# Attention on one Trainium2 core: a finished chunk's projection matmul issued right behind the matmuls of the denominators, ahead of the two copies out of PSUM

## The chip, the cores and the metric

The kernel runs on one core of a Trainium2 chip. The five engines of the core are named as in the profile: PE is the matrix engine (TensorE), with its weight loads shown apart as PEld; DVE is VectorE; ACT is ScalarE; POOL is GpSimd; SP is the queue that issues most transfers. The metric is device time in microseconds of one execution of the whole program; the time of a kernel is the median of its runs.

## The reference, cut to what matters

The program is a two-layer network on an image batch of 4 x 64 x 64 positions with 128 channels. Layer 0 is attention followed by a recurrent network over the tokens; layer 1 is a convolution with a selective scan followed by a mixture of experts. Only the attention is touched by the change. It computes, for each image `b` with its 4096 positions as a sequence, four heads of 32 channels:

```
q, k, v = split(einsum('bxyc,cf->bxyf', layernorm(x), w_qkv))
q, k    = l2norm_axis1(q), l2norm_axis1(k)
sim     = einsum('bihd,bjhd->bhij', q, k) * 10.0
attn    = softmax(sim, axis=-1)
out     = einsum('bhij,bjhd->bhid', attn, v)
out     = einsum('bxyd,dc->bxyc', out, w_out) + b_out
x       = x + out
```

So for every query position the exponentials of 4096 scores are needed for each head, their sum (the denominator), their weighted sum of `v` (the numerator), the quotient, and then a projection by `w_out`, a bias and the residual.

## The kernel before

Everything is in float32. Channels lie on the 128 partitions, so a head is a strip of 32 partitions. The kernel first normalizes and prepares `q`, `k` and `v` of the four images, stores them, and then runs the attention stage proper, `attend` (its stage of the profile lies between about 225 and 2726 us). A chunk is 512 query positions of one image; there are 8 chunks in each of 4 images, 32 in all. For each chunk the keys are walked in 32 tiles of 128 keys (`t`, up to `NJ` = 32), each with four heads (`i`). One unit is the score matmul of one tile and one head: 128 keys by 512 queries, one PSUM bank.

The stage is written under a manual schedule: each engine executes its instructions in the order in which the Python loop emits them. The loop works in turns. One turn does the following.

- `scores("sa", 4)` (L286, L301): four score matmuls into the PSUM tile `sa` (four banks, one buffer), then one exponential on ACT of all four banks (128 x 2048) into a ring in SBUF. The ring holds eight tiles of four heads.
- Either a second `scores("sb", 3)` into the PSUM tile `sb` (three banks, one buffer), with an exponential of 128 x 1536; or, in a counting turn, other use of the same `sb` tile, called `slot`.
- `weighted` (L310): for up to two finished tiles, four matmuls each that multiply the exponentials by `v` and accumulate in the PSUM bank `av`. After the last tile of a chunk ACT copies `av` to `o` (L319).
- `added` (L329, L333): DVE adds each finished tile of exponentials, 128 x 2048, to a running `total`; after eight tiles the `total` is complete and is put on the list `to_count`, due three turns later (`LATER`).
- The list `later` of the previous turn: small DVE operations whose inputs came from ACT in that turn.
- `divided` (L352, L353): when a chunk's denominators are complete, DVE takes the reciprocal and multiplies `o` by it; the chunk then goes on the list `to_project`.

A counting turn is what the change touches. `counted` (L338 to L348) issues four matmuls by a matrix of ones, one for each head, which sum `total` over the 128 keys of the partition dimension into bank 0 of `slot`; ACT then copies this bank to `den` (L345 for the first count of a chunk, L347 for the three others, whose DVE addition goes on `later`). If a chunk waits on `to_project`, the same turn calls `projected` (L355 to L366): it issues the load of the chunk's piece of `x` on the SP queue (L358), the projection matmul by `wo` of the finished `o` into bank 1 of the same `slot` (L359), and ACT's copy of that bank with the bias added (L360); the addition of the residual (L363) and the store (L364) go on `later`. The turn in which a chunk is projected is the first counting turn of the next chunk, so that its copy is the one of L345. The last chunk has no such turn: it is projected alone at the end. There are therefore 31 turns with both, and one with a projection only.

Waits between engines are put in by the framework. It follows dependencies by whole tiles: `slot` is one tile, so two accesses of it by different engines, of which one is a write, are put in the order in which they were emitted, even where they lie in different banks. In the program before, the projection matmul waits for ACT's copy of `slot`, and the biased copy waits for the projection matmul.

## Time and profile before

The kernel before takes 10372.5 us, the median of 3 runs (10369.3 to 10379.58). The profiled execution took 10381.96 us, with a span of 10379.9 us from the first instruction to the last.

| what | value |
|---|---|
| profiled execution, its span | 10381.96 us, 10379.9 us |
| median of 3 runs, lowest, highest | 10372.5 us, 10369.3 us, 10379.58 us |
| mean granted PE clock over the span | 0.966 |
| attention stage, window 240 to 2740 us: PE, DVE, ACT busy | 2340.03, 2246.10, 1970.55 us of 2500 |
| its granted PE clock | 0.99 |
| projection matmuls L359 | 64 instructions (two for each of 32 projections), 346.2 to 2722.7 us |
| copies L345 of the first count of a chunk | 32, median 578 ns |
| biased copies L360 | 32, median 689 ns |

In the lines of the profile, `L359` is a line of the kernel, the engine's name stands before it, and `out<-in` names the tiles. In the timeline a line gives the start in us, the duration in us, the instruction with the number merged into it, and in brackets the idle time of its engine before it with what ended it. `32*128` or `128*32` beside a matmul is the part of the PE array, rows by columns, that one instruction uses. A matmul in float32 appears as two PE instructions. The list of waits gives total us, times, and the longest wait.

### The profile page before, as it was taken

How to read it: one execution, taken by the hardware profiler on the slowest of the kernel's cores; microseconds unless marked ns; L12 is line 12 of the kernel's file. 1: busy time of each engine (PE TensorE's matmuls, PEld its weight loads, DVE VectorE, ACT ScalarE, POOL GpSimd, SP SyncE). 2: the span in 40 equal slices, each digit the busy share in tenths (PEclk: the TensorE clock that was granted, in tenths of full speed). 3: DMA queues.
4: the chain of work that ended last, by engine and by line, in shares of the span. 5: the costliest groups of instructions: out<-in, count | busy, mean ns of one | idle time of the engine just before them, and what ended most of it. 6: DMA issues, size and time to landing. Idle time of an engine off the chain costs nothing.

```text
span 10379.9 us, 244130 instructions
## 1 busy us (share of the span) xinstructions
PE 9318.5 (90%) x103920; PEld 4400.3 (42%) x103920; DVE 8856.0 (85%) x8023; ACT 6815.2 (66%) x9682; POOL 5616.8 (54%) x3513
## 2 busy tenths in 40 slices
PE   7999999999888869999999999999999999999766
PEld 3222222222233335555555555555555555555323
DVE  7999999999685159999999999999999999999864
ACT  3778777777564557777776776776777766767311
POOL 0000000000011159999999999999999999999300
PEclk8999999999999979999999999999999999999877
DMA  4000000000212335555655565655565555566634
GB/s 181 7 7 31 9 31 7 9 7 8 86 61 93 125 118 139 144 153 149 154 146 139 143 158 148 151 146 136 144 158 153 144 141 144 146 149 157 203 131 167
DMA packets 529249, 1173.61 MB, mean 113 GB/s; under 512 B 47954, under 2 KB 436634, under 8 KB 498330
## 3 DMA queue, kind: packets, MB, share of 16 engines
q1 hardware_dynamic: 528154, 1157.87, 40.1%
q8 instruction: 827, 13.55, 0.5%
q14 instruction: 268, 2.20, 0.1%
HBM read 816.74 MB, written 190.00 MB: 97 GB/s over the span
## 4 chain that ended last, share of the span: by engine, by line
DVE 49%; issue 8%; PE 4%; DMA 2%; DVEq 1%; POOL 0%; ACT 0%; SPq 0%; POOLq 0%; ACTq 0%
DVE states L1255 41%; DVE db L1248 3%; DVE b_diag L1139 1%; DVE log L1111 1%; PE db L1217 1%; DMA weights<-in_w 1%; PE y L1308 1%; DVEq L1255 0%; DVE y L1446 0%; PE norm_mean_ps L115 0%; PE x_ps L1065 0%; DVEq L1248 0%; PE gate_ps L1536 0%; PE pool_ps L1566 0%; PE norm_var L121 0%
## 5 line engine op out<-in xcount | busy, mean ns | idle before, releaser
L1255 DVE TENSOR_TENSOR_SCAN states<-decays,db 128x920 f32<-128x920 f32 x2304 | 4761.9, 2067 | 175.9 <-DVE db L1248 4.6
L1279 POOL TENSOR_TENSOR products<-states,c_ring 128x912 f32<-128x912 f32 x2304 | 4513.7, 1976 | 437.7 <-DVE db L1248 167.8
L1193 ACT ACTIVATE decays<-dt,a_logs 128x456 f32<-128x456 f32 x4608 | 3100.2, 676 | 97.6
L1217 PEld LDWEIGHTS db<-b_diag,dtu_t 32*128 32x128 f32 x18432 | 2233.7, 187 | 1790.5 <-issue 1332.6
L1217 PE MATMUL db<-b_diag,dtu_t 32*128 32x128 f32 x18432 | 2636.8, 282 | 374.4 <-DVE states L1255 308.7
L1217 PE MATMUL db<-b_other,dtu_t 32*128 32x128 f32 x18432 | 2674.5, 284 | 5.6 <-DMA b_other<-b_diag 3.1
L1226 PE MATMUL y<-zeros 32*128 32x128 f32 x17224 | 2496.4, 283 | 5.4 <-issue 5.3
L1308 PE MATMUL y<-products,ident 64*64 64x456 f32 x18432 | 2314.2, 570 | 9.4 <-issue 7.0
L1217 PEld LDWEIGHTS db<-b_other,dtu_t 32*128 32x128 f32 x18432 | 2236.3, 187 | 8.6 <-issue 4.7
L1226 PEld LDWEIGHTS y<-zeros 32*128 32x128 f32 x17224 | 2085.4, 187 | 7.4 <-issue 7.3
L333 DVE TENSOR_TENSOR total<-total,ring 128x2048 f32<-128x2048 f32 x768 | 1759.3, 2291 | 76.0 <-ACT ring L301 10.4
masks.py:197 POOL MEMSET ident<- 128x128 f32 x6 | 1.2, 205 | 3154.3 <-SPq L177 2840.7
L301 ACT ACTIVATE ring<-sa 128x2048 f32<-128x2048 f32 x640 | 1203.7, 1881 | 467.3 <-PE sa L286 467.3
L1266 ACT COPY carry<-states 128x8 f32<-128x8 f32 x576 | 117.7, 204 | 1677.6 <-DVE states L1255 1627.0
L310 PE MATMUL av<-ring,v_at 128*32 128x512 f32 x8192 | 1010.0, 599 | 0.1
L286 PE MATMUL sa<-q_at,k_at 32*128 32x512 f32 x5120 | 731.8, 641 | 61.2 <-ACT ring L301 36.1
L301 ACT ACTIVATE ring<-sb 128x1536 f32<-128x1536 f32 x512 | 741.4, 1448 | 0.0
L1308 PEld LDWEIGHTS y<-products,ident 64*64 64x64 f32 x18432 | 493.3, 131 | 334.5 <-issue 54.9
L286 PE MATMUL sb<-q_at,k_at 32*128 32x512 f32 x3072 | 555.3, 615 | 50.7 <-ACT ring L301 50.7
L310 PEld LDWEIGHTS av<-ring,v_at 128*32 128x32 f32 x8192 | 210.4, 109 | 700.9 <-issue 676.3
L1248 DVE COPY db<-states 128x8 f32<-128x8 f32 x1728 | 302.9, 175 | 205.8 <-PE db L1217 25.2
L286 PEld LDWEIGHTS sa<-q_at,k_at 32*128 32x128 f32 x5120 | 200.3, 183 | 616.7 <-ACT ring L301 310.0
(208 smaller groups left out, 9178.6 us busy)
## 6 DMA issues: line engine op xcount, KB each, us to landing
c_ring<-c_rows SPq DMA_DIRECT2D x576, 912.0 KB, 7.5
b_other<-b_diag SPq DMA_DIRECT2D x288, 512.0 KB, 9.6
u<-u_r SPq DMA_DIRECT2D x72, 456.0 KB, 10.4
y_r<-sum SPq DMA_DIRECT2D x72, 456.0 KB, 4.3
u<-u_c SPq DMA_DIRECT2D x72, 456.0 KB, 10.4
y_c<-sum SPq DMA_DIRECT2D x72, 456.0 KB, 4.7
weights<-in_w SPq DMA_DIRECT2D x32, 1024.0 KB, 12.9
x<-x SPq DMA_DIRECT2D x96, 256.0 KB, 2.7
```

The source lines that it names most:

```text
L286: nc.tensor.matmul(s[:, m, :], k[rows, tokens(t)], q[rows, chunk(chunk_state["c"])], start=True, stop=True,)
L301: nc.scalar.activation(ring[:, lo : lo + n, :], s[:, at : at + n, :], AF.Exp)
L310: nc.tensor.matmul(chunk_state["av"][rows, :], chunk_state["v"][:, t, rows], ring[:, at + i, :], start=t == 0, stop=t == NJ - 1,)
L333: nc.vector.tensor_add(total, total, w)
L1193: nc.scalar.activation(to, dt, AF.Exp, scale=scale)
L1217: nc.tensor.matmul(bank.rearrange("p (n t) -> p n t", n=4)[:, :, at : at + 32], v.dtu[rows, h, s, :], b[rows, s, 4 * self.q : 4 * self.q + ...
L1226: nc.tensor.matmul(y[:, idle // 2, :P], zeros[rows], zeros[rows], start=False, stop=False)
L1248: nc.vector.tensor_copy(self.edge(self.db[:, SKIP:], v.into), self.edge(before.slot(states), v.outof) if self.nth else self.carry(),)
L1255: nc.vector.tensor_tensor_scan(order(self.slot(states)), order(self.slot(decays, 1 if self.v.back else 0)), order(self.db[:, SKIP:][:, : 2 ...
L1266: nc.scalar.copy(self.carry(), self.edge(self.slot(states), self.v.outof))
L1279: nc.gpsimd.tensor_mul(to, h, c)
L1308: nc.tensor.matmul(to, ident[rows, rows], of, start=begins, stop=ends)
```

## The change

In the kernel before, one counting turn with a projection emits: four count matmuls, ACT's copy to `den`, the load of `x`, the projection matmul, ACT's biased copy. In the changed kernel it emits: four count matmuls, the load of `x`, the projection matmul, ACT's copy to `den`, ACT's biased copy. `counted` now ends after its matmuls and returns its copy as a function, `taken`; `projected` ends after its matmul and returns its biased copy as `biased`; the loop calls both after both matmuls have been emitted. A turn that only counts, and the last projection, emit the same instructions in the same order as before.

```
                 nc.tensor.matmul(
                     slot[DH * i : DH * i + DH, 0, :], ones, total[:, i, :], start=True, stop=True
                 )
+            return lambda: taken(slot, chunk_state, t)
+
+        def taken(slot, chunk_state, t):
             if t < SUMMED:
                 chunk_state["den"] = work.tile([P, 2, CH], F32, tag="den", name="den")
             den = chunk_state["den"]
...
             nc.tensor.matmul(slot[:, 1, :], wo, chunk_state["o"], start=True, stop=True)
-            nc.scalar.activation(x[:, 1, :], slot[:, 1, :], AF.Identity, bias=bo)
+
+            def biased():
+                nc.scalar.activation(x[:, 1, :], slot[:, 1, :], AF.Identity, bias=bo)
+                later.append(kept)
...
-            later.append(kept)
+            return biased
...
                 slot = ps.tile([P, 3, CH], F32, tag="sb", name="sb")
+                after = []
                 if counting:
                     _, chunk_state, t, total = to_count.pop(0)
-                    counted(slot, chunk_state, t, total)
+                    after = [counted(slot, chunk_state, t, total)]
                     if t == NJ - 1:
                         to_divide.append(chunk_state)
                 if to_project:
-                    projected(slot, to_project.pop(0))
+                    after.append(projected(slot, to_project.pop(0)))
+                for step in after:
+                    step()
```

In the built programs the order of the instructions on each single engine is the same in both kernels. What differs is the waits of 31 turns. The projection matmul no longer waits for ACT. ACT's copy to `den` now waits for the projection matmul (one more PE completion than before), and the biased copy behind it no longer waits for PE. Two waits of the following score matmuls, which the projection's old wait had covered, are now written out: `sa` on the exponential before the copy, `sb` on PE.

## The prediction

> **What bounds the kernel now.** The printed chain of work that ended last is no help for this change: it names no line of the attention stage, and its shares by engine add up to about 64% of the span. I therefore read the stage itself. The table of windows comes first: the attention stage, without its ends, in stretches of 500 us.

> ```profile
> core 0: us, PE busy (x) PEld busy (x) DVE busy (x) ACT busy (x) POOL busy (x), PEclk, DMA share, GB/s
> ...
> 500.00:1000.00 500.00, 470.60 (x3530) 125.45 (x3534) 452.21 (x220) 396.80 (x273) 0.00 (x0) 1.00 0.06 21
> ```

> PE is busy 94% of the time at full clock, DVE 90%, ACT 79%. PE leads, but DVE is close behind, so the question is whether time that PE gets back is also time that DVE has. The list of waits of the stage (240 to 2730 us) says where PE stands still for the edited lines:

> ```profile
> DVE total L329 <- ACT ring L301: 175.6, 97, 22.6
> ...
> PE sb L359 <- ACT den L345: 45.8, 31, 1.5
> ACT x_at L360 <- PE sb L359: 44.8, 32, 7.1
> ```

> PE waits 31 times for the copy to `den` before the projection, 45.8 / 31 = 1.48 us each. ACT then waits for the projection. DVE waits for exponentials about once per chunk-quarter of eight tiles, so it doesn't set the pace. Then the timeline of one engine at a time. PE in a counting turn without a projection, and in one with it:

> ```profile
> 614.44 1.14 PE L286 MATMUL sa<-q_at,k_at 32*128 32x512 f32 x8
> 615.51 1.07 PE L338 MATMUL sb<-total,ones 128*32 128x512 f32 x8
> 616.39 1.90 PE L310 MATMUL av<-ring,v_at 128*32 128x512 f32 x16
> 618.22 1.14 PE L286 MATMUL sa<-q_at,k_at 32*128 32x512 f32 x8
> ...
> 651.71 1.14 PE L286 MATMUL sa<-q_at,k_at 32*128 32x512 f32 x8
> 652.78 1.07 PE L338 MATMUL sb<-total,ones 128*32 128x512 f32 x8
> 655.33 1.12 PE L359 MATMUL sb<-o,wo 128*128 128x512 f32 x2 [1.48 <-ACT den L345]
> 656.38 1.92 PE L310 MATMUL av<-ring,v_at 128*32 128x512 f32 x16
> 658.24 1.14 PE L286 MATMUL sa<-q_at,k_at 32*128 32x512 f32 x8
> ```

> ACT, and then DVE, around the same projection:

> ```profile
> 652.92 1.88 ACT L301 ACTIVATE ring<-sa 128x2048 f32<-128x2048 f32 x1 [1.04 <-PE sa L286]
> 654.70 0.58 ACT L345 COPY den<-sb 128x512 f32<-128x512 f32 x1
> 656.49 0.69 ACT L360 ACTIVATE x_at<-sb,bo 128x512 f32<-128x512 f32 x1 [1.22 <-PE sb L359]
> 659.45 1.88 ACT L301 ACTIVATE ring<-sa 128x2048 f32<-128x2048 f32 x1 [2.27 <-PE sa L286]
> ```

> ```profile
> 660.31 0.68 DVE L363 TENSOR_TENSOR x_at<-x_at 128x512 f32<-128x512 f32 x1
> 661.36 7.08 DVE L333 TENSOR_TENSOR total<-total,ring 128x2048 f32<-128x2048 f32 x3 [0.36 <-ACT ring L301]
> 670.15 2.29 DVE L329 TENSOR_TENSOR total<-ring 128x2048 f32<-128x2048 f32 x1 [1.72 <-ACT ring L301]
> ```

> The copy cannot start before ACT has finished the exponential of 1.88 us, so PE stands behind an exponential and a copy, though it has all its data: `o` was finished by DVE's multiplication at 648.11 + 0.69 = 648.80. Everything that follows on PE, the `av` matmuls and the next `sa`, is queued behind the projection, and ACT then sits idle for 2.27 us waiting for that `sa`. From `sa` to `sa` the plain counting turn takes 618.22 - 614.44 = 3.78 us and the projecting one 658.24 - 651.71 = 6.53 us.

> [...]

> **The change part by part.** No instruction is added or removed, and on each engine the order is unchanged; the load of `x` (L358) and the store (L364) keep their places in SP's queue, where the load was issued a whole chunk ahead. The work moves only through waits.

> *The wait removed.* Eight PE instructions of the counts keep the array for about 0.88 us before the `av` matmuls follow in the plain turn (616.39 against 615.51); I take 0.86, as sixteen `av` take 1.85 us up to `sa`, with 0.13 of that for the switch to another form (24 instructions, counts and `av`, take 2.71 = 24 x 0.1075 + 0.13). The projection's switch, 128*32 to 128*128, is not in the trace; the nearest is that 0.13. It would start at 652.78 + 0.86 + 0.13 = 653.77 instead of 655.33: 1.56 us earlier. Bounds: at worst it starts when the counts have ended by the profile, 652.78 + 1.07, plus one fully exposed weight load of 0.19 (median of its row, 189 ns), 654.04, and saves 1.29. At best it starts at 653.64 and also hides the load of 0.19 that its present 1.05 us may contain, and saves 1.69 + 0.19 = 1.88.

> *What follows on PE.* `av` starts at 654.82; its exponentials were done before the counts, as the plain turn, of the same shape, runs without a wait. `sa` follows at 656.68; it needs the exponential that ends at 654.80. All this moves by the full 1.56.

> *The wait added.* ACT's copy now stands behind the projection, and behind it on ACT the biased copy and then the next exponential. The biased copy started 1.16 us after the projection (656.49 - 655.33), so the copy starts at 653.77 + 1.16 = 654.93, against 654.70 now; it costs nothing, since ACT's next exponential waits for `sa`, 656.68 + 1.21 = 657.89. Copy and biased copy, 0.58 + 0.69, are over at about 656.2. The cover is 1.7 us. The completion of the copy is now signalled together with that of the biased copy; its readers are the next count's addition and the reciprocal, turns later. The `sb` scores of the next turn need the slot free: they come at 659.20 - 1.56 = 657.64, 1.4 us after the biased copy.

> *DVE.* A chunk takes 77.30 us (578.04 to 655.33, projection to projection). Its idle time in one chunk by the timeline is 1.56 + 1.56 + 0.36 + 1.72 = 5.20 us. Behind the projection it has 0.36 + 1.72 = 2.08 before it is next held by an exponential, more than 1.56, so it can follow, with 0.5 left. Even if it fell behind, the ring gives room: in the built program the exponentials of the next turn wait for DVE additions that are over by 653.2 (650.92 + 2.28), microseconds before they are due.

> *Sum.* 31 turns x 1.56 = 48.4 us. The 32nd projection has no copy before it and gains nothing. The end of the stage, and all later stages, start that much earlier with the same instructions; I take nothing for them. Against the profiled execution: span 10379.9 - 48.4 = 10331.5, execution 10381.96 - 48.4 = 10333.6. That execution lies 9.5 us (0.09%) above the median of the runs, so for the median I give 10372.5 - 48.4 = **10324 us**. The bounds 1.29 and 1.88 give 40.0 and 58.3 us, that is 10332 and 10314.

> **The rivals.** *A, as worked out*: 10324, chance 0.87.

> *B, DVE becomes the bound.* For it: DVE is busy 90% and just before the projecting turn it runs through a reciprocal and a multiplication, without any idle time between 630 and 661 us. If its 5.20 us were needed elsewhere and only the 0.36 directly behind the turn could be used, the gain would be 31 x 0.36 = 11 us: 10361. Against it: the 1.72 us before the next L329 is plain waiting for ACT. Chance 0.05.

> *C, the wait goes but the time does not*, because another wait of the projecting turn holds PE at the old point: the counts' end, `o`, or `sa`'s own wait for its exponential. Then the time stays at 10372. Against it: `o` is 5 us early and `sa`'s exponential ends at 654.80, before 656.68. Chance 0.05, with the case that the change has no effect at all.

> *D, slower: the clock.* The gaps are rests of PE. Without them PE is busy 72.77 us of 75.74 in a chunk, 96% against 94%. If the granted clock of the stage fell for it, each 1% of clock would cost about 23.4 us (PE busy 2340.03 in 240 to 2740 us); at 2.1% the gain is used up, and from 3% on the kernel is slower by over 0.2%: at a fall to 0.96 it would take 10372.5 - 48.4 + 70 = 10394. Against it: the scan, from 3800 to 9900 us, keeps PE busy 5646.94 of 6100 us at a clock of 0.99, and where the clock is low (0.82 in 3300 to 3800 us) PE is less busy, not more. [...] Chance 0.03.

> **How the numbers follow.** About 0.2% (20.7 us) is what a measurement of this kernel tells from no change. A lies wholly beyond it; B and C lie within it; D is split, 0.01 faster and 0.02 slower. So faster 0.88, within 0.2% 0.10, slower 0.02. The range: A's bounds, 10314 to 10332, and some 7 us to either side for the scatter of the runs (10369.3 to 10379.58 before): 10308 to 10340. It leaves out B, C and D, which hold 0.13; they are within the 2 in 10 that may be left out.

> **What would show it.** In the list of waits of the stage, the wait of the projection matmul for ACT should be gone, and ACT's copy to `den` should have gained a wait for PE of some tenths of a us, 31 times; the projecting turn from `sa` to `sa` should take 4.97 us, a chunk 75.74. DVE's wait before the first L329 after a projection should shrink from 1.72 to about 0.2 to 0.5, and the idle 0.36 be gone. The end of the stage should move from 2726 to about 2678, and the later stages keep their lengths. The prediction is wrong if the matmul starts later than 654.04 in such a turn, if DVE's idle time moves but the chunk stays at 77.3, or if PEclk in 500 to 2500 us leaves 1.00.

## The result, and the profile after

The changed kernel takes 10325.78 us, the median of 5 runs (10315.29 to 10342.06), against 10372.5 us before (10365.02 to 10391.6, 5 runs): ratio 0.9956, 95% interval 0.9946 to 0.9967. It is faster by 0.44%.

The profiled execution of the changed kernel has a span of 10313.4 us, 66.5 us less than that of before. Not all of this is the change. I measure the attention loop from its first `sa` matmul to the start of its last projection matmul: before, from 238.23 to 2722.52 us, that is 2484.3; after, from 234.96 to 2671.09, that is 2436.1. So the loop gave 48.2 us. It also began 3.3 us earlier, and what lies behind it took 7642.3 us instead of 7657.4, 15 us less. These two are scatter: behind the loop, the profiled executions of the twelve rows in the table below took between 7635 and 7671 us, whatever was done to the attention.

In the line numbers of the changed kernel the projection is L362, the copy to `den` of a chunk's first count L348, the biased copy L365 and the addition of the residual L369. First the table of windows, the same stretch as before; the columns are the busy time of each engine (with the number of its instructions), and the column PEclk is the granted clock.

```profile
core 0: us, PE busy (x) PEld busy (x) DVE busy (x) ACT busy (x) POOL busy (x), PEclk, DMA share, GB/s
...
500.00:1000.00 500.00, 479.61 (x3609) 127.97 (x3606) 460.93 (x225) 406.11 (x279) 0.00 (x0) 1.00 0.06 21
```

PE is busy 96% instead of 94%, at the same clock of 1.00. Now the list of waits of 240 to 2730 us (total us, times, longest):

```profile
DVE total L329 <- ACT ring L301: 140.0, 97, 22.5
...
ACT x_at L365 <- PE sb L362: 7.1, 1, 7.1
...
PE sb L362 <- DVE o L356: 5.6, 1, 5.6
```

The wait of PE for ACT ahead of the projection, 45.8 us before, is gone from the list; what is left is the one wait of the last projection for `o`. ACT's wait for the projection fell from 44.8 us in 32 turns to 7.1 in that last one. DVE's wait at L329 fell by 175.6 - 140.0 = 35.6 us. The timeline of PE, of ACT and of DVE around one projection:

```profile
642.29 1.14 PE L286 MATMUL sa<-q_at,k_at 32*128 32x512 f32 x8
643.37 1.07 PE L338 MATMUL sb<-total,ones 128*32 128x512 f32 x8
644.36 1.12 PE L362 MATMUL sb<-o,wo 128*128 128x512 f32 x2
645.42 1.92 PE L310 MATMUL av<-ring,v_at 128*32 128x512 f32 x16
647.27 1.14 PE L286 MATMUL sa<-q_at,k_at 32*128 32x512 f32 x8
```

```profile
643.50 1.88 ACT L301 ACTIVATE ring<-sa 128x2048 f32<-128x2048 f32 x1 [1.04 <-PE sa L286]
645.52 0.59 ACT L348 COPY den<-sb 128x512 f32<-128x512 f32 x1
646.01 0.69 ACT L365 ACTIVATE x_at<-sb,bo 128x512 f32<-128x512 f32 x1
648.48 1.88 ACT L301 ACTIVATE ring<-sa 128x2048 f32<-128x2048 f32 x1 [1.78 <-PE sa L286]
```

```profile
650.89 0.69 DVE L369 TENSOR_TENSOR x_at<-x_at 128x512 f32<-128x512 f32 x1
651.50 7.08 DVE L333 TENSOR_TENSOR total<-total,ring 128x2048 f32<-128x2048 f32 x3
659.19 2.29 DVE L329 TENSOR_TENSOR total<-ring 128x2048 f32<-128x2048 f32 x1 [0.61 <-ACT ring L301]
```

The projection starts 0.99 us after the counts instead of 2.55, and from `sa` to `sa` the turn takes 4.98 us instead of 6.53. The copy waits a little for the projection, behind which ACT still has 1.78 us to spare. DVE follows: its 0.36 us are gone and its 1.72 us have become 0.61.

### The profile page after: what moved, and what is told of

Same layout as the page of the kernel before. It is cut to its first block, busy times and chain, and to the rows that moved or that the text cites. A ratio compares the mean times of both kernels' runs of the same rounds, so it can differ in the third digit from the quotient of the medians.

```text
span 10313.4 us, 244132 instructions
## 1 busy us (share of the span) xinstructions
PE 9300.8 (90%) x103920; PEld 4392.6 (43%) x103920; DVE 8853.2 (86%) x8023; ACT 6815.1 (66%) x9682; POOL 5613.4 (54%) x3513
## 4 chain that ended last, share of the span: by engine, by line
DVE 50%; issue 8%; PE 3%; DMA 2%; DVEq 1%; POOL 0%; ACT 0%; SPq 0%; POOLq 0%; ACTq 0%
DVE states L1264 42%; DVE db L1257 3%; DVE b_diag L1148 1%; DVE log L1120 1%; PE db L1226 0%; DVE y L1455 0%; DVEq L1264 0%; DVEq L1257 0%; PE pool_ps L1575 0%; PE y L1317 0%; PE norm_mean_ps L115 0%; PE gate_ps L1545 0%; DMA weights<-in_w 0%; PE norm_var L121 0%; POOL products L1288 0%
## 5 line engine op out<-in xcount | busy, mean ns | idle before, releaser
L333 DVE TENSOR_TENSOR total<-total,ring 128x2048 f32<-128x2048 f32 x768 | 1759.3, 2291 | 65.9 <-DVE total L333 2.8
L301 ACT ACTIVATE ring<-sa 128x2048 f32<-128x2048 f32 x640 | 1203.9, 1881 | 452.0 <-PE sa L286 452.0
L310 PE MATMUL av<-ring,v_at 128*32 128x512 f32 x8192 | 1010.0, 599 | 0.1
L286 PE MATMUL sa<-q_at,k_at 32*128 32x512 f32 x5120 | 731.8, 641 | 60.9 <-ACT ring L301 35.4
L301 ACT ACTIVATE ring<-sb 128x1536 f32<-128x1536 f32 x512 | 741.3, 1448 | 0.0
L286 PE MATMUL sb<-q_at,k_at 32*128 32x512 f32 x3072 | 555.3, 615 | 50.7 <-ACT ring L301 50.7
L310 PEld LDWEIGHTS av<-ring,v_at 128*32 128x32 f32 x8192 | 210.4, 109 | 700.9 <-issue 676.3
L286 PEld LDWEIGHTS sa<-q_at,k_at 32*128 32x128 f32 x5120 | 200.4, 183 | 616.4 <-ACT ring L301 309.7
```

The costliest lines, as they stand in the source:

```text
L286: nc.tensor.matmul(s[:, m, :], k[rows, tokens(t)], q[rows, chunk(chunk_state["c"])], start=True, stop=True,)
L301: nc.scalar.activation(ring[:, lo : lo + n, :], s[:, at : at + n, :], AF.Exp)
L310: nc.tensor.matmul(chunk_state["av"][rows, :], chunk_state["v"][:, t, rows], ring[:, at + i, :], start=t == 0, stop=t == NJ - 1,)
L333: nc.vector.tensor_add(total, total, w)
```

## The experiments

The theory: the gain is the stall of PE ahead of the projection, nothing else, and it reaches the end because PE sets the pace of the loop while ACT and DVE have room. The rivals: DVE is the hidden bound; ACT's pair of copies carries the gain; the order "counts first" matters for itself. The table has all runs but the last two, which had a profile and one time only. Most medians are of 5 executions; those of the kernels before with one and a half, two and three copies are of 4, 6 and 4, that of every second chunk of 21. Each ratio is taken against executions of the kernel before that were made along with that run (medians 10370.5 to 10375.9), so it can differ a little from the quotient of two rows. Loop is as defined above; chunk is the mean time from projection to projection over the first 31 projections of the profile:

| kernel | median us | ratio to before (95%) | loop us | chunk us |
|---|---|---|---|---|
| before | 10372.5 | 1 | 2484.3 | 77.30 |
| changed | 10325.78 | 0.9956 (0.9946 to 0.9967) | 2436.1 | 75.74 |
| changed, again | 10325.23 | 0.9954 (0.9941 to 0.9968) | 2436.1 | 75.76 |
| projection first | 10319.41 | 0.9948 (0.9934 to 0.9961) | 2432.7 | 75.62 |
| every second chunk | 10353.01 | 0.9980 (0.9973 to 0.9986) | 2459.8 | 76.53 |
| changed, two copies | 10319.83 | 0.9949 (0.9935 to 0.9963) | 2435.3 | 75.69 |
| before, two copies | 10411.52 | 1.0034 (1.0022 to 1.0046) | 2521.4 | 78.50 |
| changed, one more reciprocal | 10325.06 | 0.9952 (0.9939 to 0.9966) | 2437.5 | 75.75 |
| before, two more reciprocals | 10419.78 | 1.0041 (1.0027 to 1.0054) | 2520.4 | 78.39 |
| changed, two more reciprocals | 10426.06 | 1.0039 (1.0026 to 1.0053) | 2527.4 | 78.62 |
| before, one and a half copies | 10420.17 | 1.0045 (1.0028 to 1.0062) | 2521.3 | 78.46 |
| before, three copies | 10417.68 | 1.0049 (1.0032 to 1.0065) | 2524.1 | 78.58 |

The loop is the sharper measure: it came out at 2436.1 us in both profiles of the changed kernel, while whole executions of one kernel differ by 27 us.

**The changed kernel again.** No edit.

> The changed kernel once more, as the mark for the other runs on this chip. If the gain is the removed PE wait alone, 31 turns of 1.56 us: 48 us less than before, ratio 0.9953, and the attention loop itself shorter by 48 us, the stages before and after it unchanged but for scatter. If a part of the 57 to 66 us between the two profiled executions came from other stages through the change, the other stages should again be shorter by 10 us or more.

10325.23 us, and the loop to 0.1 us as in the first profile. It began at 238.08 us, as in the kernel before (238.23), so the earlier start in the first profile was not the change. Behind the loop 10319.8 - 2674.16 = 7645.6 us passed, 12 us less than before: by its letter, this is the size at which I had said that the change would be at work in other stages. The runs of the other kernels, which spread over 7635 to 7671 us with no order by kernel, speak for scatter.

**Every second chunk.**

```
                 if to_project:
+                    if to_project[0]["c"] % 2 and after:
+                        after.pop()()
                     after.append(projected(slot, to_project.pop(0)))
```

> The new order for the 16 chunks of even number whose projection falls into a counting turn, the old order for the 15 others. Theory of the PE wait: each turn counts for itself, 16 x 1.56 = 25 us less than before, ratio 0.9976, and the trace shows turns of 4.98 and of 6.53 us in alternation. Rival, DVE is the hidden bound and takes time back over several chunks: the first half of the turns would then bring nearly all of the gain, 40 us or more, as DVE would cap the sum.

The loop is 24.5 us shorter than before, against 25 expected, and the median 22.4 us below that of the executions of before made along with it. The list of waits of this kernel (240 to 2730 us) shows the stall in the 15 old turns alone, 22.2 / 15 = 1.48 us each:

```profile
PE sb L362 <- ACT den L348: 22.2, 15, 1.5
```

Turns of 4.98 and 6.52 us alternate through the whole loop. Sixteen turns bring 16 / 31 of the gain: each counts for itself, and nothing caps the sum.

**Two copies, in the changed kernel and in that of before.** The same line twice, so that ACT needs 0.6 us more in the projecting turn:

```
                 nc.scalar.copy(den[:, 0, :], slot[:, 0, :])
+                nc.scalar.copy(den[:, 0, :], slot[:, 0, :])
```

> The changed kernel with the copy to den of a chunk's first count issued twice in a row on ACT. In the changed kernel the copies stand behind the projection matmul and ACT is idle for 1.78 us after them before its next exponential. Theory (the copies are covered now): one more copy of 0.6 us costs nothing, the turn stays at 4.98 us and the time at the changed kernel's 10325. Rival (ACT's pair is itself on the path now): 31 x 0.6 = 19 us slower than the changed kernel, 10344.

> The kernel before with the copy to den of a chunk's first count issued twice in a row on ACT (the same values written twice). Theory of the PE wait: the second copy lengthens the stall of PE ahead of the projection by its own length, 0.53 to 0.58 us, in 31 turns: 16 to 18 us slower than before, 10389 to 10391, and the mean wait of the projection matmul 2.0 to 2.1 us instead of 1.48. Rival, the gain came from ACT's two copies running back to back and PE's wait is covered: no more than noise, within 5 us of before.

In the changed kernel the second copy costs nothing: the turn is 4.98 us, the loop 2435.3 us. In the kernel before it lengthens the stall to 64.9 / 31 = 2.09 us, as expected, and 18 of the 31 projecting turns to 7.14. So the ACT copy was on PE's path before and is off it now. But the cost was twice what I expected: 36 us by the medians instead of 16 to 18. In the loop it is 37.1 us, of which the longer stall accounts for 31 x 0.61 = 18.9. In the other 13 turns there is a further 1.63 us. The timeline of PE in one of these, and two windows of the same stretch (columns as in the table of windows above):

```profile
577.84 1.07 PE L338 MATMUL sb<-total,ones 128*32 128x512 f32 x8
581.00 1.78 PE L360 MATMUL sb<-o,wo 128*128 128x512 f32 x2 [2.09 <-ACT den L346]
582.71 2.91 PE L310 MATMUL av<-ring,v_at 128*32 128x512 f32 x16
```

```profile
575.00:580.00 5.00, 3.90 (x32) 0.80 (x32) 4.89 (x3) 3.96 (x4) 0.00 (x0) 1.00 0.00 0
580.00:585.00 5.00, 4.00 (x14) 0.90 (x18) 4.79 (x3) 1.60 (x3) 0.00 (x0) 0.66 0.00 0
```

Behind the stall the projection takes 1.78 us instead of 1.12 and the `av` matmuls 2.91 instead of 1.92; the granted clock of the five microseconds from 580 to 585 is 0.66 on average. Part of PE's clock was withdrawn for a while. The last experiments of this section follow that up.

**The projection first.** The projection matmul ahead of the counts, the two copies behind both:

```
                 after = []
+                if to_project:
+                    after.append(projected(slot, to_project.pop(0)))
                 if counting:
                     _, chunk_state, t, total = to_count.pop(0)
-                    after = [counted(slot, chunk_state, t, total)]
+                    after.insert(0, counted(slot, chunk_state, t, total))
                     if t == NJ - 1:
                         to_divide.append(chunk_state)
-                if to_project:
-                    after.append(projected(slot, to_project.pop(0)))
```

> The projection matmul is issued ahead of the four count matmuls, the two ACT copies follow both. Theory of the PE wait: the wait for ACT is gone here too, so at least the 48 us of the change are kept; moreover the counts and the av matmuls behind them use the same form of the array, so one switch of form per turn falls away, 0.13 to 0.2 us, 31 times: 4 to 6 us less than the changed kernel, 10319 to 10322 at the changed kernel's 10326, and from sa to sa 4.78 to 4.85 us instead of 4.98. Rival, the gain depends on the order counts first (because the copy now waits for the counts, which come last): the copy to den and the biased copy would be late, and the next exponential with them; then slower than the changed kernel.

The timeline of PE:

```profile
645.31 1.14 PE L286 MATMUL sa<-q_at,k_at 32*128 32x512 f32 x8
646.38 1.12 PE L362 MATMUL sb<-o,wo 128*128 128x512 f32 x2
647.44 1.07 PE L338 MATMUL sb<-total,ones 128*32 128x512 f32 x8
648.32 1.90 PE L310 MATMUL av<-ring,v_at 128*32 128x512 f32 x16
650.15 1.14 PE L286 MATMUL sa<-q_at,k_at 32*128 32x512 f32 x8
```

The counts are followed by `av`, which uses the array in the same form, after 0.88 us; where a switch of form follows them, in the changed kernel, it was 0.99. The turn takes 4.84 us instead of 4.98, and the loop 3.4 us less than that of the changed kernel, a little under the 4 to 6 expected. It is the best of the kernels by the loop. By whole executions, 10319.41 against 10325.23, the two can't be told apart, as their intervals overlap widely. The rival falls: the order of the two matmuls is not what matters, only that both stand ahead of the copies.

**How much room DVE has.** In `kept`, behind the addition of the residual, one or two more reciprocals whose result is not used:

```
                 nc.vector.tensor_add(x[:, 0, :], x[:, 0, :], x[:, 1, :])
+                den = chunk_state["den"]
+                for _ in range(2):
+                    nc.vector.reciprocal(den[:, 1, :], den[:, 0, :])
```

> The changed kernel with one more reciprocal of 3.35 us on DVE per chunk, right behind the addition of the residual (its result is not used). The idle time of DVE per chunk should now be 5.20 - 1.55 = 3.65 us. Theory (DVE has room left): 3.4 us fit into it, the time stays within 5 us of the changed kernel, 10325 to 10330. Rival (DVE is the bound after the change): 32 x 3.4 = 108 us slower, 10433.

> The kernel before with two more reciprocals per chunk on DVE, 6.75 us, behind the addition of the residual (results not used). The idle time of DVE there is 5.20 us per chunk. If DVE then sets the pace and can use all its idle time: 31 x (6.75 - 5.20) = 48 us slower than before, 10422. If its idle time can't be used up in this way, up to 31 x (6.75 - 2.08) = 145 us slower.

> The changed kernel with the same two more reciprocals per chunk (results not used). Theory: with 6.75 us more DVE sets the pace in both kernels, so a PE wait of 1.5 us no longer matters and the two agree within 10 us: about 10422, some 97 us over the changed kernel. Rival (PE's wait counts whatever DVE does): still 48 us below the kernel before with the same reciprocals, about 10374.

One more reciprocal, 3.35 us in each chunk, disappears in the changed kernel: 10325.06 us, a chunk 75.75 us; DVE's wait at L329 falls from 140.0 to 47.6 us. With two, both kernels come to the same time within the expected 10 us, 10419.78 and 10426.06 us, both close to the 10422 that the idle time of 5.20 us per chunk gives. The agreement with 10422 is looser than it looks: by the loop the two are 36.1 and 91.3 us longer than the same kernels without reciprocals, where 48 and 97 were expected. The stall of PE still exists in the one kernel and not in the other, but it no longer matters. The list of waits (240 to 2760 us) of the two shows where it went; first the kernel before with two more reciprocals, then the changed one:

```profile
PE sb L338 <- DVE total L333: 36.6, 32, 5.3
```

```profile
PE sb L338 <- DVE total L333: 69.5, 26, 5.3
```

The time that PE doesn't wait for the copy, 45.8 us, it now waits ahead of the counts: 69.5 us for DVE's totals, and 12.3 more that the list of the changed kernel puts down to ACT's exponentials, against 36.6. In both kernels a chunk mostly takes 78.33 us. The changed kernel's loop is still 7.0 us the longer one: it waits in fewer and longer pieces, up to 2.89 us inside the loop, and behind six of them, between 300 and 2700 us, its granted clock fell to 0.50, as in the experiments that follow. So the rival of DVE is wrong for the change as it is, but not by much: the changed kernel has some 3.6 us of DVE time left in a chunk of 75.7.

**What length of stall costs PE its clock.** The kernel before with the extra copy cut to 256 or 128 columns, or with three or four copies in a row:

```
+                nc.scalar.copy(den[:, 0, : CH // 2], slot[:, 0, : CH // 2])
                 nc.scalar.copy(den[:, 0, :], slot[:, 0, :])
```

> The kernel before with one more ACT copy of half the columns (256) ahead of the copy to den: PE's stall ahead of the projection should grow from 1.48 to about 1.8 us. The doubled copy (stall 2.09 us) cost 37 us in the loop instead of 19, as in 14 of 31 turns PE ran at half clock for a while behind the stall. Theory [...]: fewer such turns than 14, perhaps none; with none, 31 x 0.35 = 11 us slower than before. Rival (the extra copy itself, not the length of the stall, brings the slow turns): again about half of the turns with 1.6 us on top, 11 + 23 = 34 us.

> The kernel before with the copy to den issued three times in a row on ACT: PE's stall ahead of the projection should be 2.7 us. Theory (clock withdrawn by the length of the stall): more than 14 of the 31 turns run slow behind it, 20 or more, turns of about 7.75 us and of 9.4 us; 31 x 1.22 = 38 us from the stall and 33 us or more from the clock, 70 us or more slower than before. Rival (the clock has nothing to do with the length): 14 slow turns again, 38 + 23 = 61 us.

> The kernel before with one more ACT copy of a quarter of the columns (128) ahead of the copy to den: a stall of PE between 1.48 us (no slow turn in 31) and 1.9 us (16 slow turns of 31), about 1.75 us. If the length of the stall decides and the limit lies above it, no turn is slow, all take about 6.8 us and a chunk about 77.6 us; if the limit lies below it, about half of the turns take 1.6 us more.

> The kernel before with the copy to den issued four times in a row on ACT: a stall of about 3.3 us. The kernel with three copies had a longer stall than the one with two and yet only 2 slow turns instead of 14; its chunks take 78.58 us, and those of the two kernels with many slow turns 78.46 and 78.50 us on average. Theory [...]: with four copies a chunk takes 79.1 us, [...]and 10 or more of the 31 turns are slow again. Rival (the slow turns fade as the stall grows): 2 or fewer slow turns.

The expectations speak of 14 slow turns in the kernel with two copies; counted again there are 13. By the waits and the turns of each profile:

| stall of PE, mean us | 1.48 (before) | 1.8 (128 columns) | 1.88 (256 columns) | 2.09 (two copies) | 2.7 (three) | 3.3 (four) |
|---|---|---|---|---|---|---|
| slow turns of 31 | 0 | 7 | 16 | 13 | 2 | 31 |
| chunk us | 77.30 | 77.91 | 78.46 | 78.50 | 78.58 | 81.85 |

The two single executions took 10392.67 us (128 columns) and 10529.1 us (four copies), beside 10370.32 for one of the kernel before. At 256 columns I expected fewer than 14 slow turns and got 16; at three copies I expected 20 or more and got 2. The number does not simply grow with the stall. Four copies decided against the rival: the slow turns don't fade as the stall grows, all 31 are slow. But a chunk took 81.85 us and not the 79.1 that I had expected from the stall alone, since each slow turn lost more than before, about 81.85 - 79.1 = 2.75 us against 1.63 with two copies. In 29 of the turns the projection looks like this (timeline of PE):

```profile
668.91 1.06 PE L338 MATMUL sb<-total,ones 128*32 128x512 f32 x8
673.30 2.08 PE L362 MATMUL sb<-o,wo 128*128 128x512 f32 x2 [3.33 <-ACT den L348]
675.31 3.64 PE L310 MATMUL av<-ring,v_at 128*32 128x512 f32 x16
```

```profile
668.99:672.40 3.41, 0.98 (x8) 0.07 (x8) 3.20 (x3) 3.29 (x4) 0.00 (x0) 1.00 0.00 0
672.40:675.81 3.41, 2.51 (x6) 0.70 (x10) 3.31 (x2) 1.21 (x3) 0.00 (x0) 0.50 0.00 0
```

```profile
655.94:659.35 3.41, 2.33 (x20) 0.47 (x16) 3.31 (x2) 2.37 (x3) 0.00 (x0) 1.00 0.00 0
659.35:662.77 3.42, 1.79 (x10) 0.58 (x14) 3.21 (x3) 2.14 (x4) 0.00 (x0) 1.00 0.00 0
```

The two kernels differ in how much of one window the stall takes. With four copies PE is busy for 0.98 of 3.41 us, 29%, and the clock is halved for the next two windows. With three copies the stall lies across a boundary, PE is busy 68% of one window and 52% of the next, and the clock stays at 1.00. The same raster can be laid over the loop (300 to 2700 us) of every kernel in the table just above and of the two with two more reciprocals. After every window at full clock in which PE was busy less than 44% by the profile, the clock was halved; after none with more than 48% was it halved; between the two both occur. These shares were measured in these loops and do not hold behind them: in the changed kernel the window from 2734.37 to 2737.78 us had PE busy for 2.06 of 3.41 us, 60%, and the clock of the next was 0.50. The stall of 1.48 us leaves PE 57% of a window even when it lies wholly inside one.

An estimate from the 81.92 us of 24 windows: 23 are 78.51 us. Where the chunks lie against these two lengths explains the odd numbers of slow turns. With 256 columns a chunk takes 77.64 us after a fast turn and about 79.27 after a slow one, so the stall goes to and fro in the raster by 0.87 and 0.76 us, and about every second turn is slow. With three copies the chunk comes to 78.47 us by its stall alone; from the third turn on the stall moves by only 0.04 us a chunk and stays spread over two windows. That is a coincidence of this loop's length and no protection that a long stall gives. With four copies the stall begins 0.96 to 1.05 us after the start of a window in 28 of the 31 turns, and a chunk of these takes 81.92 us, 24 windows.

## Why the prediction was right

Predicted were 10324 us and a range of 10308 to 10340; measured were 10325.78. By the steps of the prediction:

- *The wait removed.* Predicted start of the projection 0.99 us after that of the counts (0.86 + 0.13 for the switch of form), measured 644.36 - 643.37 = 0.99. The nearest row for the unknown switch was the right one, and neither end of the bounds was touched. That it fits to 0.01 us is in part luck: from the counts to a matmul of the same form it is 0.88 us (616.39 - 615.51 in the kernel before, 648.32 - 647.44 with the projection first), so the first term was 0.02 too small and the switch, 0.11, as much too large. The record of the projection's weight load starts at 644.36, together with its matmul, as those of the counts (643.37) and of `av` (645.42) start with theirs; what share of the 0.99 us the load has was not shown. The copies start at 645.52, behind the end of the projection by the profile, 644.36 + 1.12 = 645.48; whether PE and ACT can use the two banks of the slot at one time was not shown either, and the new order does not need it.
- *What follows on PE.* Predicted turn 4.97 us, measured 4.98 in all 31 turns; predicted chunk 75.74, measured 75.74.
- *The wait added.* Predicted start of the copy 2.15 us after the counts (654.93 - 652.78), measured 645.52 - 643.37 = 2.15. Predicted cover 1.7 us, measured 1.78; the slot is free at 646.01 + 0.69 = 646.70, 1.5 us ahead of the next `sb` matmuls, predicted 1.4. The two-copy run shows that the cover is real. One sign that I had announced, a row of ACT waiting for PE at the copy, is not in the list; by the timeline ACT stands only 645.52 - (643.50 + 1.88) = 0.14 us there.
- *DVE.* The 0.36 us went as predicted. The 1.72 us became 0.61; I had written 0.2 to 0.5, with the addition of the residual at its full 0.69 us, while the next one starts 0.61 us after it (650.89 to 651.50). A small miss, without effect on the time.
- *Sum.* 31 x 1.56 = 48.4 us predicted, 48.2 us in the loop measured, and 46.7 us between the medians. The median fell 2 us from the forecast; with executions of one kernel 27 us apart, that closeness is luck, and the loop is the better witness. The span of the profiled execution was 18 us lower than the 10331.5 predicted; 3.3 us of that lie ahead of the loop and 15 behind it, the scatter told above.
- *The rivals.* B is excluded by the run with every second chunk and by the one reciprocal that costs nothing, C by the result itself. D, that a denser PE would lose clock, is turned round by the runs: at 96% busy the clock stayed at 1.00, and it fell to 0.50 where PE was made to wait longer: behind 7 of 31 waits at 1.8 us, behind none at 1.48. The gain carries no clock in it, since the kernel before lost none in its 31 turns (6.52 or 6.53 us each; its granted clock is 1.00 from 249.28 to 2717.11 us).

## What to carry to other kernels

Where a scheduler follows dependencies by whole tiles, two uses of one PSUM tile by different engines wait for each other in the order of emission even in different banks, here 31 times and 45.8 us in all; emitting all matmuls of a turn ahead of all copies out of it removes a round trip between engines, here 1.55 us of a turn of 6.53, without moving one instruction on any queue. Such a gain can be summed turn by turn if two things are looked up in the timeline: the cover behind the instruction that now waits, and the idle time of the next-busiest engine over a whole period. The second is also the size at which the same edit would have brought nothing, as the two reciprocals show.

## What the runs showed of the hardware

Lengthening a stall of PE can cost more than its length: 0.6 us of extra stall cost 1.2 us a turn on average (37.1 us in 31 turns), because behind 13 of the 31 stalls the granted clock was 0.50 for one window of 3.41 us. A stall of 1.8 us was enough for that in 7 turns of 31. PE was not idle for a whole window there: in these loops the clock was halved after each window of 3.41 us in which PE was busy less than 44%, and after some up to 48%. The kernel before, at 1.48 us, stood at most 0.3 us below a length at which its turns begin to lose clock. Above that length the place of the stall in the raster decided as much as the length: the kernel with three copies, at 2.7 us, lost clock in 2 turns only, the one with 256 columns, at 1.88 us, in 16.
